# Where VectorE waits for its own transpose in a recurrent step: on the next transpose, or on a memset in front of the scan

## The chip, the cores and the metric

The kernel runs on one core of a Trainium2 chip. The metric is the device time of one execution in microseconds, of which the median over the runs is given. TensorE (PE) multiplies matrices, VectorE (DVE), ScalarE (ACT) and GpSimd (POOL) work element by element, SyncE (SP) issues transfers.

## The reference

A gated recurrent layer runs over 512 steps for 8 sequences with 512 inputs and 512 units, and its output is added to the input:

```python
def step(h, x_t):
    fused = sigmoid(concatenate([x_t, h], -1) @ w_W + w_b)
    hidden_state, output_state = split(fused, 2, axis=-1)          # r, z
    memory_state = x_t @ wx_W + wx_b + hidden_state * (h @ wh_W + wh_b)
    h_new = output_state * h + (1.0 - output_state) * tanh(memory_state)
    return h_new, h_new
return x + swapaxes(scan(step, h0, swapaxes(x, 0, 1)), 0, 1)
```

Each step needs the state that the step before has made, so the 512 steps are a chain. Everything is float32.

## The kernel before

**Layout.** The 512 units lie as 4 column groups of 32 partitions. The units are split in half A and half B, each of two chunks, so that the second half can still be in work while the first half's new state already feeds TensorE. The state lies in the tiles hTA and hTB (eight of each in turn; the page leaves the numbers out).

**Matmuls.** In step i TensorE computes h times three weight matrices into three PSUM banks: bank A (192 columns: hh, z and r of half A; weights wa), bank B (128 columns: r and hh of half B) and bank C (64 columns: z of half B; weights wb). hh stands for h @ wh_W + wh_b. The order over banks and the four chunks of the state is written out by hand: "A0 B0 A1 A2 A3 B1 B2 B3 C0 C1 C2 C3", where A0, A1, B0, B1, C0, C1 read hTA, and the rest hTB. Each such item is 8 matmuls in the records, two for each of the four column groups. All matmuls come from the helper at L188. Behind these items each step places a share of the x side, eight matmuls of the program taken from a generator (`take(later, 8)`), into the banks xp; this work does not need the state. The share is cut into 192 columns, or for two of 14 blocks into twice 96, so that it is not the same in all steps.

**VectorE and ScalarE in one step.** `turned` (L377) transposes a part of a bank in blocks of 32 by 32. Per half there are three transposes: r (`turn_r`, into tr), hh (`turn_h`, L393, straight into md1A or md1B) and z (`turn_z`, into tz). ScalarE (helper `act`, L215) makes the sigmoid of r into md0A or md0B and of -z into hd0A or hd0B. A scan instruction (L361) with multiply and add then computes r * hh plus the x part into m, for each of the two chunks (`memory`); ScalarE's tanh of m goes into a slot of hTA or hTB; and a second scan per chunk (`update`) computes the new state. On VectorE the order of a step is: turn_r, turn_h, turn_z of half A, two scans of `memory` of half A, turn_r and turn_h of half B, `update` of half A chunk 0, turn_z of half B, `update` of half A chunk 1, then the rest of half B. The order on each engine is the program's (`manual_schedule`).

**Waits.** An instruction here waits for one other engine's semaphore or for VectorE's own. The first scan of `memory` of half A reads md0A, which ScalarE writes, and md1A, which VectorE itself writes in turn_h. The scan's own wait is for ScalarE. The wait for md1A is put by hand on an earlier VectorE instruction, the transpose of z of half A:

```python
tz, inst = turned("z", hf)
if hf == 0:
    tc.add_manual_dep(inst, h_done[0].name, SYNC)
```

turn_h of half A carries in the same way a wait for GpSimd.

**The small memsets.** At the end of each step three memsets of one column (L507, tile idle, IDLE = 3) stand on VectorE. Nothing reads what they write. Before them stand the transposes of the x part (`turn_x`, L255) and, in some steps, a sum of 192 columns (L477, L480). GpSimd adds the state to x into the output tile (L509).

Of the kernel before, what the change touches and what calls it, by code (L numbers as in the profile page):

```python
# [22 lines left out]
IDLE = 3  # L23
# [18 lines left out]
def tile_cond_rnn_residual(  # L42
# [39 lines left out]
    nc = tc.nc  # L82
# [83 lines left out]
    idle = const.tile([P, IDLE], F32, name="idle")  # L166
# [47 lines left out]
    def act(key, out_, in_, func, **kw):  # L214
        inst = nc.scalar.activation(out_, in_, func, **kw).ins  # L215
        if key in written:
            tc.declare_no_dep(inst, written[key], reason="ordered through VectorE")
        written[key] = inst
        return inst
# [114 lines left out]
    for i in range(T):  # L334
# [40 lines left out]
        def turned(n, hf):  # L375
            t_ = work.tile([P, 2, 32], F32, tag=f"t{n}{hf}", name=f"t{n}{hf}_{i}")
            inst = nc.vector.transpose(t_.rearrange("p c n -> p (c n)"), raw[n][hf]).ins  # L377
            return t_[:, :, rows], inst
# [19 lines left out]
                tc.add_manual_dep(inst, pool_done[i + 1 - NH].name, SYNC)  # L398

        def turn_z(hf):  # L400
            tz, inst = turned("z", hf)
            if hf == 0:
                tc.add_manual_dep(inst, h_done[0].name, SYNC)
            act(
                ("zc", hf, i % 2),
                hd0[hf][i % 2][:, :, :, 2].rearrange("p n c -> p c n"),
                tz,
                AF.Sigmoid,
                scale=-1.0,
            )  # L410
# [17 lines left out]
        turn_r(0)  # L428
        turn_h(0)
        turn_z(0)  # L430
        memory(0, 0)
        memory(0, 1)
        turn_r(1)
        turn_h(1)
        update(0, 0)
        turn_z(1)
        tc.add_manual_dep(update(0, 1), r_done[1].name, SYNC)
        if i == 0:
# [64 lines left out]
            weight_sum(1 if i < 5 else 3, *divmod((i - 1) % 4, 2))  # L503
        if i == 4:
            nc.gpsimd.tensor_tensor(step_bias, bias[:, BE[1]], bias[:, AL[1]], ALU.subtract)
        for n in range(IDLE):
            nc.vector.memset(idle[:, n : n + 1], 0.0)  # L507
        def add(hf, engine):
            return engine.tensor_tensor(  # L509
# [98 lines left out]
```

## Time and profile before

| | |
|---|---|
| runs, median of 3 | 1675.38 us (1673.64 to 1677.71) |
| profiled execution | 1671.65 us, its span 1669.3 us |
| TensorE busy | 1655.0 us, 99% of the span |
| VectorE busy | 1102.7 us, 66% |
| ScalarE busy | 956.9 us, 57% |
| transpose tz<-A | 511 of 250 ns |
| transposes tr<-A, md1A<-A | 511 each of 250 and 209 ns |
| memset idle | 1536 of 59 ns |
| granted TensorE clock | 1.0 |

Times are of one profiled execution; L377 is line 377 of the kernel before. In a row of the timeline stand the start in us, the duration in us, the engine, the line, the operation, the tiles out<-in, their shapes and the number of instructions merged; in brackets the idle time before it and what ended that. Rows of several instructions overlap the next ones. In the list of waits stand who waited, for whom, the total in us, the number of waits and the longest.

### The profile page before, as it was taken

What the parts mean: (1) busy time and instruction counts of PE and PEld (TensorE: products, weight loads), DVE (VectorE), ACT (ScalarE), POOL (GpSimd) and SP (SyncE); (2) the same over time, 40 slices, a digit from 0 to 9 for tenths busy, and PEclk for the clock granted to TensorE, in tenths of its full rate; (3) what the DMA queues carried; (4) which work ended last, traced back from release to release, by engine and by line L of the source; (5) the groups of instructions that cost most, each with busy time, mean ns of one, the idle gap of its engine ahead of it and who ended that gap; (6) DMA issues with size and microseconds to landing.
All of it is one profiled execution on the core that took longest, in us unless ns stands there. A gap on an engine that the chain in (4) does not pass through costs nothing.

```text
span 1669.3 us, 131859 instructions
## 1 busy us (share of the span) xinstructions
PE 1655.0 (99%) x57230; PEld 1504.4 (90%) x57230; DVE 1102.7 (66%) x9387; ACT 956.9 (57%) x5822; POOL 300.5 (18%) x1281
## 2 busy tenths in 40 slices
PE   8999999999999999999999999999999999999998
PEld 5999999999999999999999989999899999999997
DVE  6666666666666666666666666666666666666666
ACT  3555555555555555555555555555555555555555
POOL 1111111111111111111111111111111111111111
PEclk9999999999999999999999999999999999999999
DMA  4000000000000000000000000000000000000000
GB/s 179 17 11 12 18 18 18 17 5 18 17 18 18 5 18 18 17 17 5 18 18 17 18 17 5 18 17 17 18 5 18 17 18 18 5 17 12 11 11 11
DMA packets 11533, 31.53 MB, mean 19 GB/s; under 512 B 1220, under 2 KB 1732, under 8 KB 10824
## 3 DMA queue, kind: packets, MB, share of 16 engines
q1 hardware_dynamic: 10800, 22.94, 3.9%
q8 instruction: 448, 7.34, 1.8%
q14 instruction: 133, 1.09, 0.2%
q10 hardware_dynamic: 152, 0.16, 0.0%
HBM read 14.70 MB, written 8.39 MB: 14 GB/s over the span
## 4 chain that ended last, share of the span: by engine, by line
PE 97%; DMA 1%; DVE 1%; issue 0%; ACT 0%; SPq 0%
PE A L188 40%; PE B L188 26%; PE xp L188 18%; PE C L188 13%; DMA wb<-in_wb_dram 1%; DMA wx<-in_wx_dram 0%; DVE tr L377 0%; DVE tz L377 0%; DVE hTA L361 0%; DVE m L361 0%; DVE md1A L393 0%; DVE md1B L393 0%; ACT hTB L215 0%; ACT xp L223 0%; DVE hTB L361 0%
## 5 line engine op out<-in xcount | busy, mean ns | idle before, releaser
L188 PE MATMUL A<-wa,hTA 128*32 128x192 f32 x8176 | 536.1, 328 | 2.8 <-DVE hTA L361 2.8
L188 PE MATMUL A<-wa,hTB 128*32 128x192 f32 x8176 | 435.6, 326 | 0.1
L188 PE MATMUL B<-wb,hTA 128*32 128x128 f32 x8192 | 429.5, 273 | 0.8 <-DMA wb<-in_wb_dram 0.8
L377 DVE STREAM_TRANSPOSE tr<-A 128x64 f32<-128x64 f32 x511 | 127.7, 250 | 435.6 <-PE A L188 435.6
L509 POOL TENSOR_TENSOR ot<-xin,hTB 128x16 f32<-128x16 f32 x503 | 125.5, 250 | 1324.8 <-DVE hTB L361 1314.1
L188 PEld LDWEIGHTS B<-wb,hTA 128*32 128x32 f32 x8192 | 307.5, 122 | 37.6 <-DMA wb<-in_wb_dram 1.1
L215 ACT ACTIVATE md0A<-tr 128x16 f32<-128x16 f32 x512 | 112.7, 220 | 397.6 <-DVE tr L377 397.6
L188 PEld LDWEIGHTS A<-wa,hTB 128*32 128x32 f32 x8176 | 292.3, 122 | 45.7 <-DVE hTB L361 0.7
L188 PE MATMUL B<-wb,hTB 128*32 128x128 f32 x8192 | 327.1, 273 | 0.1
L188 PEld LDWEIGHTS A<-wa,hTA 128*32 128x32 f32 x8176 | 263.9, 123 | 37.5 <-DVE hTA L361 22.4
L188 PEld LDWEIGHTS B<-wb,hTB 128*32 128x32 f32 x8192 | 249.6, 122 | 0.3 <-DMA wb<-in_wb_dram 0.3
L361 DVE TENSOR_TENSOR_SCAN hTB<-hd0B,hTB 128x24 f32<-128x24 f32 x1024 | 157.7, 195 | 100.5 <-ACT hTB L215 100.3
L188 PE MATMUL C<-wb,hTB 128*32 128x64 f32 x8192 | 218.6, 219 | 1.0 <-issue 1.0
L188 PE MATMUL C<-wb,hTA 128*32 128x64 f32 x8192 | 217.9, 219 | 0.0
L188 PEld LDWEIGHTS C<-wb,hTA 128*32 128x32 f32 x8192 | 195.4, 122 | 0.0
L361 DVE TENSOR_TENSOR_SCAN hTA<-hd0A,hTA 128x24 f32<-128x24 f32 x1024 | 191.0, 186 | 0.0
L188 PE MATMUL xp<-tw,sx 128*32 128x192 f32 (+1 forms) x3472 | 186.1, 303 | 0.3 <-issue 0.2
L215 ACT ACTIVATE hd0B<-tz 128x16 f32<-128x16 f32 x512 | 114.9, 224 | 110.7 <-DVE tz L377 110.7
L215 ACT ACTIVATE hd0A<-tz 128x16 f32<-128x16 f32 x512 | 115.1, 225 | 101.3 <-DVE tz L377 101.3
L188 PEld LDWEIGHTS C<-wb,hTB 128*32 128x32 f32 x8192 | 167.2, 122 | 0.9 <-issue 0.8
L215 ACT ACTIVATE hTB<-hTB 128x16 f32<-128x16 f32 x512 | 120.3, 235 | 78.7 <-DVE hTB L361 63.2
L215 ACT ACTIVATE hTB<-m 128x8 f32<-128x8 f32 x1024 | 160.6, 206 | 0.0
(91 smaller groups left out, 2281.5 us busy)
## 6 DMA issues: line engine op xcount, KB each, us to landing
xin<-in_x_dram SPq DMA_DIRECT2D x31, 256.0 KB, 3.0
out_dram<-ot SPq DMA_DIRECT2D x31, 256.0 KB, 2.2
wx<-in_wx_dram SPq DMA_DIRECT2D x4, 768.0 KB, 6.8
wa<-in_wa_dram SPq DMA_DIRECT2D x4, 384.0 KB, 8.8
wb<-in_wb_dram SPq DMA_DIRECT2D x1, 1152.0 KB
wb<-in_wb_dram SPq DMA_DIRECT2D x1, 384.0 KB, 11.2
out_dram<-ot SPq DMA_DIRECT2D x1, 192.0 KB, 1.9
head<-in_xh_dram ACTq DMA_DIRECT2D x1, 144.0 KB, 4.8
```

The costliest lines, as they stand in the source:

```text
L188: nc.tensor.matmul(out_, lhsT, rhs, start=start, stop=False, skip_group_check=True)
L215: inst = nc.scalar.activation(out_, in_, func, **kw).ins
L361: return nc.vector.tensor_tensor_scan(*[t_[:, :, c_].rearrange("p n c s -> p (n c s)") for t_ in (out_, d0, d1)], 0.0, ALU.mult, ALU.add,).ins
L377: inst = nc.vector.transpose(t_.rearrange("p c n -> p (c n)"), raw[n][hf]).ins
L509: return engine.tensor_tensor(ot[:, t, 2 * hf : 2 * hf + 2, :].rearrange("p c n -> p n c"), x_of(c, slice(2 * hf, 2 * hf + 2), t, 1).rearr ...
```

## The change

One of the three memsets of each step is moved from the step's end to a place between the transpose of z of half A and the first scan of half A, and the wait for the transpose of hh of half A is put on that memset. The transpose of z of half A has no wait left. The number of instructions on each engine stays the same. On VectorE, step 195 is, in order, before: tr, md1A [waits for GpSimd], tz [waits for VectorE], scan m [waits for ScalarE]; after: tr, md1A [waits for GpSimd], tz, memset [waits for VectorE], scan m [waits for ScalarE].

```diff
         def turn_z(hf):
-            tz, inst = turned("z", hf)
+            tz, _ = turned("z", hf)
             if hf == 0:
+                inst = nc.vector.memset(idle[:, IDLE - 1 :], 0.0).ins
                 tc.add_manual_dep(inst, h_done[0].name, SYNC)
...
-        for n in range(IDLE):
+        for n in range(IDLE - 1):
             nc.vector.memset(idle[:, n : n + 1], 0.0)
```

## The prediction

> **What bounds the kernel now.** I read the page first, then the waits, the timeline of single steps engine by engine, and the starts in the trace's records to the nanosecond.
>
> ```profile
> PE 1655.0 (99%) x57230; PEld 1504.4 (90%) x57230; DVE 1102.7 (66%) x9387; ACT 956.9 (57%) x5822; POOL 300.5 (18%) x1281
> ```
>
> TensorE looks full, so a nanosecond on VectorE counts only where TensorE really waits for VectorE. The waits name one such place: the first weights of a step, the state of half A.
>
> ```profile
> DVE tr L377 <- PE A L188: 435.6, 510, 1.7
> PEld A L188 <- DVE hTA L361: 22.4, 119, 0.4
> ```
>
> VectorE waits for bank A of every step, then TensorE sometimes waits for the state made from it. Together that is a ring: bank A, the transposes, the scans, hTA, bank A of the next step. The starts of tr<-A show two lengths of a step. In undisturbed steps they are 3.270 us for i mod 8 = 0, 1, 4, 5 ("heavy": 16 matmuls of 192 columns for x) and 3.125 us for 2, 3, 6, 7 ("light": half of these cut to 96 columns, 8 full and 8 half). TensorE in a heavy step, then in two light ones:
>
> ```profile
> 809.68 0.83 PE L188 MATMUL xp<-wx,xin 128*32 128x192 f32 x16
> 810.33 0.51 PE L188 MATMUL A<-wa,hTA 128*32 128x192 f32 x8
> 810.66 0.40 PE L188 MATMUL B<-wb,hTA 128*32 128x128 f32 x8
> ...
> 812.95 0.68 PE L188 MATMUL xp<-tw,sx 128*32 128x192 f32 x16
> 813.44 0.53 PE L188 MATMUL A<-wa,hTA 128*32 128x192 f32 x8
> 813.79 0.40 PE L188 MATMUL B<-wb,hTA 128*32 128x128 f32 x8
> ...
> 816.57 0.52 PE L188 MATMUL A<-wa,hTA 128*32 128x192 f32 x8
> 816.91 0.40 PE L188 MATMUL B<-wb,hTA 128*32 128x128 f32 x8
> ```
>
> From the start of xp to that of A it is 0.65 us heavy and 0.49 light, 0.16 less work; but the step is only 0.145 shorter. The rest is lost at A: A to B takes 0.33 us after heavy x work, 0.34 to 0.35 after light. To the nanosecond, four matmuls of 192 columns (one row of the array's four column groups) follow each other every 162 ns, and so do A's two rows in a heavy step; in a light step they are 178 to 180 apart. So TensorE waits some 17 ns in a light step, and none in a heavy one.
>
> The last ten steps have no x work, and yet the same 3.125 us: there the ring alone sets the time, and TensorE stands still:
>
> ```profile
> 1656.22 0.55 PE L188 MATMUL A<-wa,hTA 128*32 128x192 f32 x8 [0.28 <-DVE hTA L361]
> ```
>
> Now VectorE and ScalarE inside the ring, in one light step:
>
> ```profile
> 815.23 0.25 DVE L377 STREAM_TRANSPOSE tr<-A 128x64 f32<-128x64 f32 x1 [0.83 <-PE A L188]
> 815.41 0.21 DVE L393 STREAM_TRANSPOSE md1A<-A 128x64 f32<-128x64 f32 x1
> 815.65 0.25 DVE L377 STREAM_TRANSPOSE tz<-A 128x64 f32<-128x64 f32 x1
> 815.82 0.24 DVE L361 TENSOR_TENSOR_SCAN m<-md0A,md1A 128x16 f32<-128x16 f32 x2
> ```
> ```profile
> 815.52 0.22 ACT L215 ACTIVATE md0A<-tr 128x16 f32<-128x16 f32 x1 [0.76 <-DVE tr L377]
> 815.93 0.23 ACT L215 ACTIVATE hd0A<-tz 128x16 f32<-128x16 f32 x1 [0.20 <-DVE tz L377]
> 816.05 0.30 ACT L215 ACTIVATE hTA<-m 128x8 f32<-128x8 f32 x2
> ```
>
> tz is the transpose of z that carries the wait. In ns from the start of tr, medians: tr 0 to 250; md1A (hh) 174 to 382; tz 415 to 666; scan m 590 to 739; tr of half B 740; md1B 892 to 1100; first update hTA 1053 to 1260; TensorE's weight load 1314. On ScalarE: sigmoid of r 283 to 505; sigmoid of z 700 to 925; first tanh 823 to 1020.
>
> **What the change does to the ring.** Prices from these rows:
>
> - Without a wait, VectorE starts the next instruction 76 to 83 ns before the recorded end of the last (tr to md1A: 174 after a 250 ns one; tr of B to md1B: 151 after 227). tz starts 33 ns *after* md1A's end, because it waits for it. Without that it starts at 382 - 77 = 305, 110 earlier.
> - ScalarE follows an end on VectorE by 33 ns (250 to 283, 666 to 700), VectorE an end on ScalarE by 34 (1020 to 1053, the first update). So tz ends at 555 and sigmoid of z starts at 588 instead of 700; ScalarE is free then (505).
> - The memset comes behind tz, at 305 + 174 = 479. The transpose it waits for was seen done at 382 + 33 = 415: the wait is met. Its cost as an instruction: the three idle memsets are recorded at 59 ns each and 0.08 us together, 8 ns from start to start; where three of them stood between two transposes that waited for nothing long (at 22.4 us), the second began 122 ns after the first where two bare transposes of that shape are 98 apart: 24 for three. I take 8; bounds are 0 and the recorded 59. Behind it in the queue stands the scan, with all of half B's work after it.
> - The scan waits for the sigmoid of r: 505 + 34 = 539. Behind the memset it could start at 487 (538 at the upper bound), so 539 holds in any case: 51 earlier than 590. This is what is late next. The cover is 60 ns (479 to 539): a memset of the recorded 59 just fits, and one nanosecond more would cost one.
> - From there on VectorE's own pace: scan + 69 + 82 + 151 puts md1B at 841, the update at 841 + 132 = 973. ScalarE: the tanh starts after sigmoid of z (588 + 123 = 711) or after the scan (539 + 149 + 33 = 721), ends 197 later at 918, and lets the update go at 952. So 973 instead of 1053: hTA is 80 ns earlier (29 if the scan did not move). The transpose from bank B has its data (matmuls end near 465, seen about 67 later); z of half B comes to 1098, and bank C ends at 1034 + 67 = 1101, so half B moves by some 79 as well.
> - One memset fewer at the step's end: 8 ns before a wait of 0.6 to 1.0 us for bank A. Nothing. No DMA moves, and no queue is passed.
>
> **The sum.** A heavy step gains nothing: TensorE comes to A at 1339, behind its own x work, and hTA was ready for 1314. A light step needs hTA 17 ns earlier to be full, has 80, and then TensorE is the bound: 3125 - 17 = 3109 (check: 3270 less two rows at 162 for two at 82 is 3110). Of 248 light steps between i = 5 and 500, 218 are undisturbed: 218 x 16.5 = 3.6 us. In the other 30 TensorE lost more for other reasons, and a stall behind bank A already hides the 17; half of them, 0.25 us. Ten steps at the end and the last chain gain the whole 80: 11 x 0.08 = 0.9 us. Together 4.7 us. The profiled execution took 1671.65 us (span 1669.3), so 1666.9; the median of the runs is 1675.38, 0.2% above it, and gives 1670.7. Two medians can be told apart from about 0.2%, 3.4 us: my gain is just above that.
>
> **A rule against it.** The rows say that a wait on VectorE's own work costs 110 ns and a tiny memset 8. The Trainium skill speaks the other way: by "VectorE: DVE Perf Modes", The DRAIN you can't avoid, a semaphore costs nothing over the pipeline's own flush and only the number of instructions counts; by "Perfetto Trace Analysis", Optimizing Scalar/DVE Operations, an instruction on SBUF has about 60 ns of overhead. By these two the change would take away nothing and add an estimated 60 ns, and the kernel would be slower by some 9 us.
>
> **Rivals.** *The memset is the loss* (slower). tz does not move, and the memset takes its recorded 59 ns between tz and scan: scan at 649, update at 649 + 302 + 132 = 1083, 30 late. Light and last steps lose it whole (258 x 30 = 7.7 us); heavy ones have 25 to spare and lose 5 (1.2 us): 1684.3. It decides from 29 ns of memset where tz stays (the update had 1053 - 1024 to spare), from 140 where tz moves as I say (479 to 619). Against it: the overlap at 174 and 151, and the 24 ns for three. For it: no row has a memset with a wait in front of an instruction that is free to go. Chance 0.08.
>
> *The 17 ns are TensorE's own* (same). If A's second row is late after a short x row whatever hTA does, only the last steps gain: 0.9 us, 1674.5. For it: I read the 17 ns off starts of pipelined matmuls, and no light step here had hTA early. Against: light steps whose last x row is full (i mod 8 = 3, 7) have the same 178, and second rows come 204 ns after the first weight load in light steps and in the empty last ones alike, as a late load would make it. With gains of my kind that fall under 0.2%: chance 0.2.
>
> **How the numbers follow.** My forecast, faster, has 0.72. Its bounds are 253 x 18 + 11 x 82 ns = 5.5 us and 3.4, so 1669.9 to 1672.0; the runs scatter by 2 us about their median. The range takes in the rival without a gain and that scatter, 1667.8 to 1675.8, and leaves out the slower one.
>
> **What would show it.** In the changed profile: tz 0.13 us behind md1A instead of 0.24, and no idle time of VectorE before it; ScalarE's wait for tz of half A down from 101.3 us to about 43; scan m at 0.54 us behind tr; hTA at 0.97; light steps 3.109 us, A to B 0.33 in every step; heavy steps still 3.270; the last steps 3.045. I am wrong if tz moves and light steps stay at 3.125 (the second rival), or if the scan starts later than 0.59 (the first).

## The result, and the profile after

Over 20 runs of each, the changed kernel takes 1674.76 us and the kernel before 1676.95 us in the median. The medians are 2.2 us apart. The ratio on record, which is not the quotient of the two medians, is 0.9984 with a 95% interval of 0.9976 to 0.9992. So it is faster, by 2.7 us by that ratio (1.3 to 4.0). This is less than the 4.7 us of the prediction, and under the 0.2% from which it held two medians to be distinct.

The profiled execution of the changed kernel happens to be the longest of its 20 (1678.11 us, span 1675.8; before, 1671.65 and 1669.3). The gain is therefore read from single steps. First the waits; columns as before.

```profile
DVE tr L377 <- PE A L188: 459.8, 511, 1.6
PEld A L188 <- DVE hTA L361: 4.3, 11, 0.4
```

TensorE's weight loads waited for hTA 119 times before; now 11 times, and ten of these are the steps at the end. VectorE waits longer for bank A instead. Then TensorE in two light steps:

```profile
816.41 0.57 PE L188 MATMUL A<-wa,hTA 128*32 128x192 f32 x8
816.74 0.46 PE L188 MATMUL B<-wb,hTA 128*32 128x128 f32 x8
...
819.52 0.57 PE L188 MATMUL A<-wa,hTA 128*32 128x192 f32 x8
```

From A to B it is 0.33 us, as in heavy steps. The undisturbed light steps are 3109 to 3110 ns (3125 before), the heavy ones 3270 as before, and the last ten, where the ring alone decides, 3079 (3124 before). These two lines are the starts of two of them:

```profile
1658.45 0.25 DVE L377 STREAM_TRANSPOSE tr<-A 128x64 f32<-128x64 f32 x1 [0.84 <-PE A L188]
1661.53 0.25 DVE L377 STREAM_TRANSPOSE tr<-A 128x64 f32<-128x64 f32 x1 [0.94 <-PE A L188]
```

VectorE and ScalarE in one light step of the changed kernel:

```profile
818.21 0.25 DVE L377 STREAM_TRANSPOSE tr<-A 128x64 f32<-128x64 f32 x1 [0.87 <-PE A L188]
818.38 0.21 DVE L393 STREAM_TRANSPOSE md1A<-A 128x64 f32<-128x64 f32 x1
818.52 0.21 DVE L377 STREAM_TRANSPOSE tz<-A 128x64 f32<-128x64 f32 x1
818.68 0.06 DVE L403 MEMSET idle<- 128x1 f32 x1
818.75 0.28 DVE L361 TENSOR_TENSOR_SCAN m<-md0A,md1A 128x16 f32<-128x16 f32 x2
```
```profile
818.50 0.22 ACT L215 ACTIVATE md0A<-tr 128x16 f32<-128x16 f32 x1 [0.79 <-DVE tr L377]
818.76 0.23 ACT L215 ACTIVATE hd0A<-tz 128x16 f32<-128x16 f32 x1
818.98 0.31 ACT L215 ACTIVATE hTA<-m 128x8 f32<-128x8 f32 x2
```

tz begins 0.14 us behind md1A (0.24 before). To the nanosecond, from the start of tr: tz 305 to 512, memset 468, first scan 535 to 727, second scan 644 (108 behind the first, 69 before), md1B 880, first update 1011 (1053 before). So the update starts 42 ns earlier, not 80; it is also recorded some 4 ns shorter (1011 to 1215, before 1053 to 1260), so hTA is ready 45 ns earlier. The groups by form show where the other half went:

```profile
L377 DVE STREAM_TRANSPOSE tz<-A 128x64 f32<-128x64 f32 x511 | 105.9, 207 | 0.0
L361 DVE TENSOR_TENSOR_SCAN m<-md0A,md1A 128x16 f32<-128x16 f32 x1024 | 142.1, 181 | 4.3
L215 ACT ACTIVATE hd0A<-tz 128x16 f32<-128x16 f32 x512 | 115.9, 226 | 21.8
```

The idle time ahead of tz (17.7 us before) is gone, and tz itself is 207 ns instead of 250. ScalarE's wait for tz (101.3 us before) is down to 21.8. The two scans have become longer in return, 181 ns in the mean instead of 157.

### The profile page after: what moved, and what is told of

Same layout as the page of the kernel before. It is cut to its first block, busy times and chain, and to the rows that moved or that the text cites. A ratio compares the mean times of both kernels' runs of the same rounds, so it can differ in the third digit from the quotient of the medians.

```text
span 1675.8 us, 131859 instructions
## 1 busy us (share of the span) xinstructions
PE 1659.2 (99%) x57230; PEld 1600.1 (95%) x57230; DVE 1092.3 (65%) x9387; ACT 1029.6 (61%) x5822; POOL 302.1 (18%) x1281
## 4 chain that ended last, share of the span: by engine, by line
PE 97%; DMA 1%; DVE 1%; issue 0%; ACT 0%; SPq 0%
PE A L188 40%; PE B L188 26%; PE xp L188 18%; PE C L188 13%; DMA wb<-in_wb_dram 1%; DMA wx<-in_wx_dram 0%; DVE tr L377 0%; DVE m L361 0%; DVE tz L377 0%; DVE hTA L361 0%; DVE md1B L393 0%; DVE md1A L393 0%; ACT hTB L215 0%; SPq L125 0%; DVE hTB L361 0%
## 5 line engine op out<-in xcount | busy, mean ns | idle before, releaser
L188 PE MATMUL A<-wa,hTA 128*32 128x192 f32 x8176 | 567.1, 327 | 2.4 <-DVE hTA L361 2.3
L188 PE MATMUL B<-wb,hTA 128*32 128x128 f32 x8192 | 469.2, 273 | 0.8 <-DMA wb<-in_wb_dram 0.8
L188 PEld LDWEIGHTS B<-wb,hTA 128*32 128x32 f32 x8192 | 361.4, 122 | 8.2 <-DMA wb<-in_wb_dram 1.1
L188 PE MATMUL B<-wb,hTB 128*32 128x128 f32 x8192 | 347.0, 273 | 1.4 <-DMA wb<-in_wb_dram 1.4
L188 PEld LDWEIGHTS A<-wa,hTB 128*32 128x32 f32 x8176 | 332.0, 122 | 12.5 <-DVE idle L508 0.4
L188 PEld LDWEIGHTS A<-wa,hTA 128*32 128x32 f32 x8176 | 309.5, 122 | 20.2 <-DVE hTA L361 4.3
L188 PE MATMUL C<-wb,hTB 128*32 128x64 f32 x8192 | 240.0, 220 | 3.4 <-issue 3.2
L188 PE MATMUL C<-wb,hTA 128*32 128x64 f32 x8192 | 238.1, 219 | 0.0
L188 PEld LDWEIGHTS C<-wb,hTA 128*32 128x32 f32 x8192 | 215.5, 122 | 0.2
L215 ACT ACTIVATE hd0B<-tz 128x16 f32<-128x16 f32 x512 | 115.4, 225 | 101.3 <-DVE tz L377 101.3
L215 ACT ACTIVATE hTA<-m 128x8 f32<-128x8 f32 x1024 | 160.7, 206 | 0.0
## 6 DMA issues: line engine op xcount, KB each, us to landing
wb<-in_wb_dram SPq DMA_DIRECT2D x1, 384.0 KB, 12.5
```

The costliest lines, as they stand in the source:

```text
L188: nc.tensor.matmul(out_, lhsT, rhs, start=start, stop=False, skip_group_check=True)
```

## The experiments

All edits are against the kernel before or the changed kernel. The kernel before took from 1673 to 1706 us in the different series; the five series behind the first ran on five different chips. So each kernel is compared with the runs of the kernel before in its own series alone. "Regular" or "undisturbed" is a step of the length that its kind has when TensorE does not stall; "stalls" are the time over these lengths, summed over the profile. Their counts move by a few with the tolerance that is allowed.

### What a memset does to the scan behind it

**m1**, against the changed kernel: the wait goes back to tz, the memset stays in front of the scan.

```diff
-            tz, _ = turned("z", hf)
+            tz, inst = turned("z", hf)
             if hf == 0:
-                inst = nc.vector.memset(idle[:, IDLE - 1 :], 0.0).ins
                 tc.add_manual_dep(inst, h_done[0].name, SYNC)
+                nc.vector.memset(idle[:, IDLE - 1 :], 0.0)
```

> The wait stays on the transpose of z, as before; only one memset is moved in front of the scan. Times in ns from the start of tr of half A; the changed kernel showed its memset at 468, the first scan at 535, the second 108 later (before: 69), the first update at 1010. Theory C (cold start): the 39 ns are lost because the scan now starts on ScalarE's release; a memset alone costs 8. Here the scan is behind tz and not behind ScalarE (released at 539): scan near 597, second scan 69 later, update at 1053 as before, because ScalarE's tanh still sets it; light steps 3125, heavy 3270, last steps 3124. Theory M (memset): a memset makes the scan behind it slow wherever it stands: second scan 108 behind the first, update at 597 + 108 + 85 + 151 + 131 = 1072; light and last steps near 3145. The slower rival of the prediction: update at 1083, light and last steps 3155, heavy 3275.

Measured: first scan 599, second 103 behind it, update 1070; regular light steps 3138, heavy 3270, last steps 3135. A single run of each gave 1708.84 us beside 1705.7 for the kernel before, a difference that single runs cannot carry. Its timeline and one of its groups:

```profile
800.80 0.25 DVE L377 STREAM_TRANSPOSE tz<-A 128x64 f32<-128x64 f32 x1
800.98 0.19 DVE L361 TENSOR_TENSOR_SCAN m<-md0A,md1A 128x16 f32<-128x16 f32 x1
801.00 0.06 DVE L404 MEMSET idle<- 128x1 f32 x1
801.08 0.17 DVE L361 TENSOR_TENSOR_SCAN m<-md0A,md1A 128x16 f32<-128x16 f32 x1
```
```profile
L361 DVE TENSOR_TENSOR_SCAN m<-md0A,md1A 128x16 f32<-128x16 f32 x1024 | 139.3, 178 | 0.0
```

Theory C falls as it was put: a memset alone, in front of a scan that waits for nothing (no idle time ahead of it), makes the first scan 186 ns long instead of 149 and lets the second follow 34 ns later. The memset's recorded start (801.00) lies behind that of the scan it precedes in the program, so these starts of memsets are not the time they take in the queue.

**k8 and k24**, against the changed kernel: 8 or 24 more memsets behind the one that waits (the lines are those of k8; k24 has 24 for 8).

```diff
                 tc.add_manual_dep(inst, h_done[0].name, SYNC)
+                for n in range(8):
+                    nc.vector.memset(more[:, n : n + 1], 0.0)
```

> The changed kernel with eight more memsets of one column behind the one that waits, in front of the scan. Theory C: each costs 8 ns, the scan comes at 487 + 64 = 551, past ScalarE's release at 539, so it is not cold: second scan 69 behind it, update at 551 + 302 + 132 = 985, 25 earlier than in the changed kernel in spite of eight more instructions; last steps 3079 - 25 = 3054, light steps 3110 and heavy 3270, because TensorE sets them. Theory M: scan near 599, second scan 108 behind, update near 1074; light steps near 3148, last steps near 3143, heavy near 3288.

> The changed kernel with 24 more memsets in front of the scan, to see where the ring decides. Theory C: scan at 487 + 192 = 679, update at 679 + 302 + 132 = 1113, 60 later than in the kernel before: light and last steps 3125 + 60 = 3185, heavy steps 3270 + 60 - 25 = 3305, the whole kernel some 28 us slower than the changed one. Theory M: update from 1150 to 1190, light steps 3225 to 3265. If light steps were not set by the ring (the prediction's second rival), they would stay at 3110.

Measured, k8: first scan 560, second 104 behind, update 1032; light steps 3111, heavy 3270, last steps 3100; a single run 1704.7 us beside 1705.7. k24: first scan 772, second 108 behind, update 1248; light steps 3315, heavy 3314, last steps 3314; a single run 1742.01 us.

Neither theory has the size. From k8 to k24 the update moves by 216 ns for 16 memsets, so one takes 13.5 ns of the queue, not the 8 between their recorded starts. With that the scan's place comes out: tz at 305 leaves the queue after 131 (as md1A does), one memset makes 449, nine make 557 (measured 560), 25 make 773 (772). And the second scan is 104 to 108 behind in both, though ScalarE's release at 539 is past: a memset in front is enough. The ring is confirmed: the update 21 ns later than in the changed kernel (k8) costs light and heavy steps nothing and the last steps 21; the update 195 ns later than in the kernel before (k24) makes every step 3125 + 195 = 3320 by the ring, and 3315 was measured (the update is 203 ns long here, 208 in the kernel before, which is the difference).

**c1**, against the changed kernel: the wait is carried by a one-column copy.

```diff
-                inst = nc.vector.memset(idle[:, IDLE - 1 :], 0.0).ins
+                inst = nc.vector.tensor_copy(idle[:, IDLE - 1 :], zeros[:, :1]).ins
```

> The wait is carried by a copy of one column (it reads memory, a memset does not) in place of the memset. Known from the runs so far: a memset alone, with nothing to wait for, makes the next scan some 39 ns longer in its slot (second scan 103 behind the first instead of 69). In the changed kernel the scan also waits for ScalarE (released at 539). Theory W: a wait that is not met in time does the same by itself, so the scan starts near 535 and the second 108 behind it, and the first update stays at 1010. Theory M alone: only a memset does it; the scan starts at 539, the second 69 behind, the update at 972. Light steps 3110 and heavy steps 3270 by both, last steps 3079 or 3045; time as in the changed kernel within 0.4 us.

```profile
800.47 0.14 DVE L403 COPY idle<-zeros 128x1 f32<-128x1 f32 x1
800.57 0.28 DVE L361 TENSOR_TENSOR_SCAN m<-md0A,md1A 128x16 f32<-128x16 f32 x2
```

Measured: first scan 535, 192 long, second 108 behind, update 1011; steps 3110, 3270 and 3079, all as in the changed kernel. Ratio 0.9982 (0.9962 to 1.0003). So theory W fits: no memset stands there, and the second scan is late by the same amount, behind a wait for ScalarE that is not yet met. That a one-column copy could do the same as a memset is not excluded by this run alone; but the updates in the kernel before show it without either. The first, which nothing but a wait for ScalarE precedes, is 208 ns long with 125 to the next start; the second chunk's, with its wait long met, has 165 and 86. In a step of the kernel before:

```profile
800.37 0.21 DVE L361 TENSOR_TENSOR_SCAN hTA<-hd0A,hTA 128x24 f32<-128x24 f32 x1
800.49 0.23 DVE L377 STREAM_TRANSPOSE tz<-C 128x64 f32<-128x64 f32 x1
800.64 0.17 DVE L361 TENSOR_TENSOR_SCAN hTA<-hd0A,hTA 128x24 f32<-128x24 f32 x1
800.73 0.25 DVE L361 TENSOR_TENSOR_SCAN m<-md0B,md1B 128x16 f32<-128x16 f32 x2
```

### How much of the ring TensorE leaves to be won

**even_before and even_after**: x work in equal shares of 336 columns a step (SHARE), on the kernel before and on the changed one. The generator now hands over a whole share at a time, so a step takes one.

```diff
             for k in range(2):
-                w = HALF // 2 if (2 * n + k) % 7 == 3 else HALF
-                for c0 in range(0, HALF, w):
+                c0 = 0
+                while c0 < HALF:
+                    w = min(HALF - c0, SHARE - used)
...
+                    if used == SHARE:
+                        used = 0
                         yield
...
-            take(later, 8)
+            take(later, 1)
```

> The kernel before with the wait where it was, but with TensorE's x work cut into equal shares: 336 columns in each step in place of 384 or 288, the same matmul work in more and smaller pieces. Theory of the prediction (ring 3125, TensorE's work 3270 or 3110): every step is then bound by TensorE at the mean, (3270 + 3110) / 2 = 3190, and the ring never decides while there is x work. So it wins what the change wins in light steps, 248 x 16 ns = 4.0 us, without touching the wait; the last ten steps stay at 3124. If TensorE lost the 17 ns by itself after short x work, steps would come to 3198 and nothing would be won. A cost of the ten pieces in place of eight per four steps would show as steps over 3190.

> The equal shares together with the moved wait. Theory: steps at 3190 as with equal shares alone, because the ring, now near 3080, has nothing to decide; only the last ten steps are shorter, 3079 instead of 3124, 0.5 us in all. If the moved wait helped TensorE in another way than through light steps, the difference to equal shares alone would be as large as in the change, 0.16%.

Measured: 1.0315 (1.0287 to 1.0344) and 1.0309 (1.028 to 1.0339), 50 us slower. Of 491 steps with x work 190 and 185 have the 3190 ns that were expected, in both kernels, so an undisturbed step is TensorE's alone; the others are longer, because TensorE stalls, and the waits name no other engine for it ("issue"; in even_before 26.4 us of TensorE's weight loads for C and 25.0 of those for xp).

As a way to win the 4 us it is a miss: the kernels with more and smaller matmuls (3% more) are slower by twelve times that. The two kernels differ by 0.06% (last steps 3124 and 3079, as expected), but within intervals of 0.6%.

**uncut_before and uncut_after**: the other way round, x work in whole blocks, six steps of two blocks and two of one.

```diff
-                w = HALF // 2 if (2 * n + k) % 7 == 3 else HALF
+                w = HALF
...
-            take(later, 8)
+            take(later, 4 if i % 8 in (3, 7) else 8)
```

> The kernel before with its x work in whole blocks of 192 columns: per eight steps six of two blocks and two (i mod 8 = 3, 7) of one, in place of four of two and four of one and a half. The wait is where it was. Theory (ring 3125, TensorE's work 3270 for two blocks, 3270 - 325 = 2945 for one): six steps of 3270 and two of 3125 that the ring sets, 290 ns more per eight steps, 62 x 0.29 = 18 us over the kernel before in regular steps; if TensorE's stalls go with the number of matmuls, which falls by 3%, some of it comes back.

> The same with the moved wait. Theory: the one-block steps are set by the ring in both, so here the whole shortening of the ring is seen, 3125 to 3079 as in the last ten steps, not the 16 ns that TensorE left of it in the change: 124 x 46 + 10 x 45 ns = 6.2 us faster than the uncut kernel with the wait on the transpose, a ratio of 0.9964 between the two. If the gain of the change came from elsewhere, it stays near 3 us here too, and one-block steps do not shorten by 46.

Measured, in one series with the kernel before at 1673.43 us: 1682.81 us, ratio 1.0055 (1.004 to 1.0069), and 1676.69 us, ratio 1.0016 (1.0007 to 1.0026). Between them 6.1 us, where 6.2 was expected. Against the kernel before the loss is 9.4 us, where 18 was expected of regular steps; fewer stalls are the likely reason, but the kernel before was not profiled in this series. The starts of a one-block step and the next, without and with the moved wait:

```profile
809.36 0.25 DVE L377 STREAM_TRANSPOSE tr<-A 128x64 f32<-128x64 f32 x1 [0.74 <-PE A L188]
812.48 0.25 DVE L377 STREAM_TRANSPOSE tr<-A 128x64 f32<-128x64 f32 x1 [0.59 <-PE A L188]
```
```profile
807.01 0.25 DVE L377 STREAM_TRANSPOSE tr<-A 128x64 f32<-128x64 f32 x1 [0.80 <-PE A L188]
810.09 0.25 DVE L377 STREAM_TRANSPOSE tr<-A 128x64 f32<-128x64 f32 x1 [0.60 <-PE A L188]
```

3.12 us becomes 3.08 (medians 3124 and 3078), two-block steps stay at 3270. The moved wait is worth 46 ns where TensorE has nothing else to do, and in the change only the 16 that its work leaves. The uncut kernels also lose almost nothing to stalls: the time over the regular lengths sums to 1.3 and 0.4 us, with 10 and 6 disturbed steps.

**halfcut_after**: the moved wait, and one block cut in two.

```diff
-                w = HALF // 2 if (2 * n + k) % 7 == 3 else HALF
+                w = HALF // 2 if 2 * n + k == 3 else HALF
...
-            take(later, 8)
+            take(later, 4 if i % 8 == 3 else 8)
```

> The moved wait, with one of the 14 blocks of x work cut in two instead of two (before and the change) or none (uncut): per eight steps five of two blocks at 3270, two of one and a half at 3110, one of one block at the ring's 3079, and 60 matmuls of the program for x instead of 64 or 56. Theory: regular steps cost (5 x 3270 + 2 x 3110 + 3079) - (4 x 3270 + 4 x 3110) = 129 ns more per eight steps than in the changed kernel, 8.0 us in all. Stalls of TensorE added 8 to 40 us with 64 matmuls and 0.4 to 1.3 us with 56. If they grow evenly with the number, half of them is left, and the kernel comes within 5 us of the kernel before on either side; if they appear only at the full number, it beats the changed kernel where that has more than 8 us of them.

Measured: 1686.42 us, the kernel before 1694.65 us, ratio 0.9949 (0.9931 to 0.9967). Steps 3270, 3110 and 3080 as expected; 21 us over the regular lengths. The kernel before had 36 us of it in the one profile from a series of like length. So it beats the kernel before clearly, and by more than the changed kernel did in two series of like length (0.998 and 0.9985); the two were not run side by side. That fewer stalls do it is the likely reason, since its regular steps cost 8.0 us more than those of the changed kernel and so would alone make it slower than the kernel before; the stalls of the two were not compared in one series.

### The change once more, and the kernel before against itself

> The changed kernel once more, beside the two with equal shares. By the steps of the profile it should win 248 x 16 + 10 x 45 ns = 4.4 us where no step is disturbed, ratio 0.9974; a stall of TensorE behind bank A hides the 16 ns of its step, so with 30 to 60 disturbed light steps 3.4 to 3.9 us, ratio 0.9977 to 0.998. If stalls became more frequent with the change, the sum of the time over the regular lengths of steps in the profiles of changed kernels would be higher than the 8 to 13 us of before.

> The kernel before against itself, to see what the comparison tells from no change, and its profile beside that of the changed kernel on the same chip. Regular steps 3125, 3270 and 3124 as ever; ratio 1.000. If stalls of TensorE do not depend on the change, some 80 to 90 of the 248 light steps are disturbed, as in the three kernels that were profiled in the first runs of this series, and the regular ones lose 16.5 ns each at bank A: some 160 x 16.5 = 2.6 us.

> The changed kernel beside it. With some 160 regular light steps it wins 160 x 16 ns = 2.6 us, 0.45 in the last ten steps, and in the disturbed light steps, of which half had their stall ahead of bank A, some 0.4: 3.4 us, ratio 0.998. The prediction's sum with 218 regular steps and 80 ns gave 0.9972.

Measured: the changed kernel 0.998 (0.9964 to 0.9995) and, in another series, 0.9985 (0.9965 to 1.0004); the kernel before against itself, in the latter series, 0.9995 (0.9977 to 1.0012). That series can't show a gain of this size: the medians of the kernel before against itself are 1699.21 and 1702.24 us, 3.0 apart with no change at all, and after_third has 1698.86. The gain rests on the first series and on after_again, whose intervals leave out 1, on the uncut pair, and on the lengths of the steps. The profile of before_again has 167 regular light steps and 36 us of stalls, those of the changed kernel 167 and 39 (after_again), 174 and 37 (after_third). In the first series it was 9 us before and 17.5 in the changed kernel, a short execution of the one and the longest of the other. So there is no sign that the change makes TensorE stall more where both were profiled at like length; the stalls differ from execution to execution and from series to series.

## Why the prediction was right in kind, and where its size was off

**Right.** The ring and its place; the wait costing 110 ns of tz's start (415 to 305); heavy steps at 3270; light steps bound by TensorE at 3110 (3109 forecast); the memset hidden by ScalarE's release (535 against 539 expected); half B and bank C not becoming late. The rival that the 17 ns are TensorE's own is out: light steps lost 16. The rival that the memset is the loss is out for the change, but its mechanism is half real: in m1, where nothing hides it, the memset makes the update start 17 ns later and a regular light step 13 longer.

**Off: the scan's price.** The step "from there on VectorE's own pace: scan + 69 + 82 + 151" took over the durations of a scan that follows its predecessor without a break (149 ns, next start 69 later). Behind a wait that is not met, or behind a memset, it is 192 and 108. Those 39 ns are the 38 by which the update is later than forecast (1011 for 973): in m1, k8, k24, c1 and the changed kernel alike it starts 131 ns behind md1B, on VectorE's own pace. But ScalarE's path, forecast to let the update go at 952, was mis-sized by nearly as much: the tanh starts 34 behind the longer scan, at 761 (721 forecast), takes 213 ns (197 forecast) and ends at 975, which lets the update go at about 1008. So a scan that let its successor follow after 69 ns would alone have brought no more than 3 ns; its length and the tanh's count too. In the same way tz was put at 250 ns, the length it had behind its wait; without it tz is 207, and sigmoid of z starts at 546, not 588, which brought nothing, since the tanh waits for the scan. Of the 80 ns 42 are left at the update's start and 45 at its end; the light steps needed 17, and so only the last steps show it: 45 each, 0.5 us in place of 0.9. The memset too was under-priced, 8 ns for 13.5, which ScalarE's release at 539 hid.

**Off: the number of steps that gain.** 218 undisturbed light steps of 248 were counted in one profile, and its execution was 5 us shorter than the median of 20. In before_again, of a later series, 167 are left, and 167 x 16 = 2.7 us.

**Off: the start.** The prediction took the first steps as unchanged. In step 0 the first update of hTB starts 0.1 us behind its tanh in the kernel before and 0.5 us in the changed one, m1 and c1, an idle time that the waits in the profile do not explain; step 6 begins 0.3 us later for it (41.24 us in after_again, 40.95 in before_again). In two of the three profiles of the changed kernel, and in k8, the last of wb also landed 1.3 us later (12.5 us from issue, 11.2 before; 12.1 in k24), and step 6 began 2.6 us later; in neither profile of the kernel before. But step 6 begins as late as 42.7 us in uncut_before too (40.9 in both profiles of the kernel before), where the wait is as before, the first steps have the same program and wb landed after 11.1 us. So starts differ by about 2 us without the change as well. Whether the late landing comes with the change was not settled; it is not in the sum.

For the first series I estimate, from its median and the two profiles of the kernel before, some 210 regular light steps: 3.4 us, with 0.2 for disturbed ones and 0.5 for the last ten, less 0.3 at the start. That is 3.8 us, inside the measured 1.3 to 4.0; what lies between 3.8 and the middle of the interval stays open.

**The rule that spoke against it.** By the Trainium skill ("VectorE: DVE Perf Modes", The DRAIN you can't avoid) a semaphore costs nothing over the pipeline's flush; the same section adds that an instruction that is not held starts earlier, which the prediction left out. The trace agrees with the addition and not with the first: the wait cost 110 ns of tz's start, because tz otherwise starts 77 ns before the end of its predecessor. The 60 ns per instruction of "Perfetto Trace Analysis", Optimizing Scalar/DVE Operations, are near the 59 ns that a memset's record shows here, but not what it takes of the queue: 13.5 ns for a memset, and 34 to 39 once for the instruction behind it.

## What to carry to other kernels

An engine's wait for its own last result belongs where that engine will wait for another anyway; put it on an instruction whose start others depend on, and the overlap of two instructions is lost as well as the wait. Price a moved instruction with the duration it has in its new place: behind an unmet wait it is the row of a like instruction behind a wait that counts, not its own row from before. Do so on every path that meets there: here a path that was forecast 21 ns ahead came within 3 ns of the bound. What a shorter ring brings is capped in each step by the other engine's own work, so count steps by kind, and count the regular ones in more than one profile.

## What the runs showed of the hardware

- The first VectorE instruction behind an unmet wait is recorded some 43 ns longer (scan 192 for 149, transpose 250 for 207, update 208 for 165), and the next one starts some 39 ns later (108 for 69 behind the scan, 125 for 86 behind the update); a memset of one column in front does nearly the same to a scan that waits for nothing (186 and 103).
- A row of one-column memsets takes 13.5 ns each of VectorE's queue (k8 and k24), although their recorded starts are 8 ns apart and can lie behind the start of the next instruction.
- TensorE's stalls without a named releaser were larger in kernels with more matmuls: with 64 matmuls of the program for x per eight steps 9 to 43 us from series to series, with 60 21 us and with 56 0.4 to 1.3 us in one series each, and with more and narrower ones the kernel took 50 us more. Number and width were always changed together, and the series differ, so whether the number or the narrow ones do it, and how much, is open.
